# Two places of one recurrent block exchanged: the first norm's statistics go to ScalarE, the bonus goes back to a product of its own

## The chip, the cores and the metric

The program runs on one core of one Trainium2 chip. The metric is device time in microseconds (us) of one execution; times are medians of several runs. The engines are called as the profile calls them: PE (TensorE, with PEld for its weight loads), DVE (VectorE), ACT (ScalarE), POOL (GpSimd) and SP (SyncE, which here issues DMAs only).

## The reference

The kernel computes one RWKV-6 block on 32 sequences of 128 tokens and 512 features, all in float32. Cut to what matters:

```python
xn = layernorm(x)                         # the first norm: mean and variance over 512 features
sx = token_shift(xn)                      # previous token minus this one
xxx = tanh((xn + sx*maa_x) @ maa_w1)      # five small projections
x5 = xn + sx*(maa_stack + xxx @ maa_w2)   # five mixed inputs
w = exp(-exp(time_decay + tanh(x5[1] @ decay_w1) @ decay_w2))
r, k, v, g = x5[3] @ Wr.T, x5[0] @ Wk.T, x5[2] @ Wv.T, silu(x5[4] @ Wg.T)
for t in tokens:                          # 32 heads of 16 x 16 state
    a = k_t[:, None] * v_t[None, :]
    out_t = r_t @ (u * a + s)             # u*a is the "bonus" of the present token
    s = a + w_t[:, None] * s
x = x + (head_norm(out) * g) @ Wo.T
# then a second layernorm, token shift and a squared-ReLU feed-forward with a sigmoid gate
```

## The kernel before, in words

The 32 sequences are worked in eight groups of four (NG = 8, GB = 4), so a group has 512 token columns (N). Each group passes through these streams, which are Python generators:

- front_mix: loads x, runs the first norm (layernorm_T, called with sums None), transposes it on PE, and makes the five mixed inputs x5. The weight products of the mixing are L427, and their evictions are L486 with L488 on POOL, or L491 with L493 on DVE alone.
- front_proj and front_gate: the decay, then k, r, v (matmuls of L408, evictions of L562 on ACT, each with DMAs that put one head's channel on each partition) and the gate (L583 on ACT, L585 on DVE).
- prep: prepares the recurrence on DVE: the rows rk and a10 of the bonus (L660 to L680), the states, and the decays over pairs of tokens. The recurrence steps over pairs of tokens, 64 steps instead of 128.
- The recurrence streams. For each half of the value channels (dh, two of them) and each of the 16 key channels q there is one unit, so 32 units a group: ACT copies the decays into sc (L705) and the start state into a (L716); POOL makes the products am of k and v (L730) and adds them by pairs (L734); DVE runs the scan over time (L768) and multiplies by r into rm (L770); PE adds rm into acc by eight transposing matmuls (L797), a "set". When a half is done, ACT copies acc to y (L811).
- back: head norm, gate and output projection (L885), the sum with x (L894, which also sums rows for the second norm's mean), the second norm (layernorm_T called with sums: a Square pass with an accumulator on ACT, L354, and the normalising pass L368), its transposes and evictions (L394, L384, L905, L908), and the feed-forward (L408 again for its first product, L959, L975).

The statistics of the first norm, for every group, are made on DVE: BN_STATS (L339) and BN_AGGREGATE (L340) for each of the four sequences. After them, for both norms, DVE makes variance plus epsilon (L357, rstd), POOL raises it to the power -0.5 (L359), DVE makes the offset nb (L361), and ACT applies both (L368).

The bonus is made on DVE by bonus_rows: v times rk (L750), v times a10 (L753), and their sum on every second token (L757). In the first and last group the result is a 17th product rm that PE adds as one more set. In groups 1 to 6 ("within") DVE adds it to the rm of the last key channel (L775), so PE has 16 sets for each half.

The order of instructions on each engine is decided when the program is built, by class Plan. It runs all streams together: at each step it takes, among the next operations of all streams that could start earliest by its own estimates (within the tolerance EPSILON), the one with the earliest due time. A stream's due times run in a line from g + v0 to g + v1, and the pairs (v0, v1) stand in DUE. Each operation gives the planner its engine, an estimated duration, and what it reads, writes and allocates; buffers are rings with a few slots (two of rm, two of sc, two of a, one of am, four of blk, four of ps in PSUM). On the chip each engine executes its queue in order, and semaphores make it wait for the others. DMAs are issued on SP's and ACT's queues, so an ACT instruction can stand behind a DMA issue.

Of the kernel before, what the change touches and what calls it, by code (L numbers as in the profile page):

```python
# [10 lines left out]
AF = mybir.ActivationFunctionType  # L11
ALU = mybir.AluOpType
AX = mybir.AxisListType

P = 128
B, L, E = 32, 128, 512
# [4 lines left out]
NG = B // GB  # L21
# [21 lines left out]
LANDING = 2.0  # L43
HOP = (0.2, 0.05, 0.05, 0.04, 0.08)
ON_POOL = (2, 3, 4)
EPSILON = 0.022


DUE = {"rec": (-0.102, 1.125), "mix": (-6.405, -3.209), "proj": (-7.732, 7.646), "gate": (-1.235, 1.547), "prep": (-2.764, -0.303), "back": (-0.938, 3.79), "last1": (-28.476, 2.758), "last2": (7.398, 21.019)}


class Buf:
# [130 lines left out]
def rwkv6_block(ctx: ExitStack, tc: tile.TileContext, x, prev, s0, vecs, u, maa_w1, maa_w2,  # L183
# [94 lines left out]
    def pair(ap):  # L278
        return ap.rearrange("p c (n j) -> p c n j", j=2)
# [46 lines left out]
    def layernorm_T(g, src, sums, vw, vb, which, use, take, need=None, bs=range(GB)):  # L326
# [3 lines left out]

        b0, nb_ = bs[0], len(bs)
        bsl, cols = slice(b0, b0 + nb_), slice(b0 * L, (b0 + nb_) * L)
        if sums is None:
            xh = src
            stats, mv = yield Op(DVE, 0.88, r=[(src, b0)], w=[(0, b0), (1, b0)], alloc=["stats", "mv"])
            for b in bs:
                if b != b0:
                    yield Op(DVE, 0.88, r=[(src, b)], w=[(stats, b), (mv, b)])
                nc.vector.bn_stats(stats[:, b, :], src[:, b, :])  # L339
                nc.vector.bn_aggr(mv[:, b, :], stats[:, b, :])  # L340
            stats.open = False
            mean, var, scale = mv[:, bsl, 0], mv[:, bsl, 1], 1.0
        else:
            mv = sums
            yield Op(DVE, 0.16, r=[(mv, b) for b in bs], w=[(mv, "m")])
            mean, var, scale = mv[:, bsl, 0], mv[:, bsl, 1], 1.0 / E
            nc.vector.tensor_scalar(mean, mean, -1.0 / E, None, ALU.mult)
            xh = None
            for b in bs:
                if xh is None:  # L350
                    (xh,) = yield Op(ACT, 0.83, r=[(src, b), (mv, "m")], w=[(0, b), (mv, ("v", b))], alloc=["ev"])
                else:
                    yield Op(ACT, 0.83, r=[(src, b), (mv, "m")], w=[(xh, b), (mv, ("v", b))])
                nc.scalar.activation(xh[:, b, :], src[:, b, :], AF.Square, bias=mv[:, b, 0:1],  # L354
                                     accum_out=mv[:, b, 1:2])
# [2 lines left out]
        yield Op(POOL, 1.1, r=[(rstd, None)], w=[(rstd, None)], port=True)  # L358
        nc.gpsimd.tensor_tensor(rstd[:, bsl], rstd[:, bsl], mhalf[:, bsl], ALU.pow)  # L359
        (nb,) = yield Op(DVE, 0.16, r=[(mv, None), (rstd, None)], w=[(0, None)], alloc=["nb"], port=True, end=[mv])  # L360
        nc.vector.scalar_tensor_tensor(nb[:, bsl], mean, -1.0 if sums is None else 1.0, rstd[:, bsl], ALU.mult, ALU.mult)  # L361
        for b in bs:
            if g == 0 and sums is None and b % 2:
                yield Op(DVE, 0.5, r=[(src, b), (nb, None), (rstd, None)], w=[(xh, b)], port=True)
# [373 lines left out]
    def rec_dve(gs):  # L738

        for g in gs:  # L740
            d = data[g]
            yield Op(DVE, 0.0, need=lambda: "w01" in d and ("v", "all") in d)
            r, v = d["r"], d["v"]
            r2, v2 = pair(r.t), pair(v.t)
            for dh in range(NDH):
                ds = slice(dh * DH, (dh + 1) * DH)
                def bonus_rows():
                    yield Op(DVE, 0.0, need=lambda: "a10" in d)
                    (rm,) = yield Op(DVE, 1.2, r=[(v, None), (d["rk"], None)], w=[(0, None)], alloc=["rm"], port=True)
                    nc.vector.tensor_tensor(rm.t, v[:, ds, :], d["rk"].t.unsqueeze(1).to_broadcast([P, DH, L]), ALU.mult)  # L750
                    (am,) = yield Op(DVE, 0.67, r=[(v, None), (d["a10"], None)], w=[(0, None)], alloc=["ps"], port=True)
                    bo = am.t.rearrange("p (d n) -> p d n", n=T2)
                    nc.vector.tensor_tensor(bo, v2[:, ds, :, 0], d["a10"].t.unsqueeze(1).to_broadcast([P, DH, T2]),  # L753
                                            ALU.mult)
                    yield Op(DVE, 0.67, r=[(am, None)], w=[(rm, None)], end=[am])
                    rm2 = pair(rm.t)
                    nc.vector.tensor_tensor(rm2[:, :, :, 1], rm2[:, :, :, 1], bo, ALU.add)  # L757
                    return rm

                within = 0 < g < NG - 1  # L760
                for q in range(S):
                    if within and q == S - 1:
                        rows = yield from bonus_rows()
                    yield Op(DVE, 0.0, need=lambda: (g, dh, q, "sum") in unit and (g, dh, q, "sc") in unit)
                    a, sc = unit[g, dh, q, "a"], unit[g, dh, q, "sc"]
                    yield Op(DVE, 1.22, r=[(a, None)], w=[(sc, None)], end=[a])
                    scf = sc.t.rearrange("p d n -> p (d n)")
                    nc.vector.tensor_tensor_scan(scf, scf, a.t.rearrange("p d n -> p (d n)"), 0.0, ALU.mult, ALU.add)  # L768
                    (rm,) = yield Op(DVE, 1.21, r=[(sc, None), (r, None)], w=[(0, None)], alloc=["rm"], end=[sc])
                    nc.vector.tensor_tensor(  # L770
                        pair(rm.t), sc.t.unsqueeze(3).to_broadcast([P, DH, T2, 2]),
                        r2[:, q : q + 1, :, :].to_broadcast([P, DH, T2, 2]), ALU.mult)
                    if within and q == S - 1:
                        yield Op(DVE, 1.2, r=[(rows, None)], w=[(rm, None)], port=True, end=[rows])
                        nc.vector.tensor_tensor(rm.t, rm.t, rows.t, ALU.add)  # L775
                    unit[g, dh, q, "rm"] = rm
                if not within:
                    unit[g, dh, S, "rm"] = yield from bonus_rows()
            r.open = v.open = d["rk"].open = d["a10"].open = False

    def rec_pe(gs):

        for g in gs:
            d = data[g]
            for dh in range(NDH):
                acc = None
                last = S - 1 if 0 < g < NG - 1 else S
                for q in range(last + 1):
                    yield Op(PE, 0.0, need=lambda: (g, dh, q, "rm") in unit)
                    rm = unit[g, dh, q, "rm"]  # L790
                    if acc is None:
                        (acc,) = yield Op(PE, 0.875, r=[(rm, None)], w=[(0, None)], alloc=["acc"], end=[rm])
                    else:
                        yield Op(PE, 0.875, r=[(rm, None)], w=[(acc, None)], end=[rm])
                    for i in range(DH):

                        nc.tensor.matmul(acc[:, i, :], lhsT=rm[:, i, :], rhs=by_head, is_transpose=True,  # L797
                                         start=(q == 0 and i % 4 == 0), stop=(q == last), skip_group_check=True)
                unit[g, dh, "acc"] = acc

    def rec_out(gs):
# [234 lines left out]
```

## Time and profile before

| | us |
|---|---|
| median of three runs | 1539.01 |
| lowest and highest run | 1536.59, 1539.5 |
| profiled execution, own time | 1536.59 |
| its span, first to last instruction | 1534.8 |
| PE busy in the span | 1401.9 (91%) |
| DVE busy | 1276.1 (83%) |
| POOL busy | 1033.6 (67%) |
| ACT busy | 650.9 (42%) |

The profile is one execution, and its times are from the span's start. The mean granted clock of PE was 0.96. "Busy" of PE includes matmuls that overlap in its pipeline, so means of one matmul are longer than the distance between two of them. Register, semaphore and DMA-issuing instructions are not counted as busy.

### The profile page before, as it was taken

The page shows a single profiled execution, that of the slowest core. Times are in us where ns is not written, and L with a number is a line of the kernel's source. Part 1 is how long each engine was busy: PE and PEld are TensorE (multiplying, and loading weights), DVE is VectorE, ACT ScalarE, POOL GpSimd, SP SyncE. Part 2 cuts the span into 40 slices and gives each one's busy share as a digit, 9 for nine tenths or more (in the row PEclk, how much of TensorE's full clock was granted, in tenths as well). Part 3 has the DMA queues.
Part 4 walks back from the last instruction along what each step waited for, and adds up shares of the span by engine and source line. Part 5 has one row for each costly group of instructions (what it writes and reads, how often), then busy time and mean ns, then how long its engine had stood idle before and what let it go on. Part 6 is the DMA issues. An engine that isn't in the chain of part 4 may idle for free.

```text
span 1534.8 us, 16413 instructions
## 1 busy us (share of the span) xinstructions
PE 1401.9 (91%) x5248; PEld 736.2 (48%) x5248; DVE 1276.1 (83%) x1626; ACT 650.9 (42%) x1271; POOL 1033.6 (67%) x642
## 2 busy tenths in 40 slices
PE   5897898889999999999999989999899989779778
PEld 2344454454544555454544545455544555355444
DVE  6529899889989899989989888989989898978742
ACT  3243252324733265434633265424743354245252
POOL 4227895784868958685868949586876959579600
PEclk9998998799999999999999999999999999889889
DMA  6121421343315421442205430243314420410220
GB/s 223 55 86 36 130 69 32 129 128 99 103 32 171 145 89 42 134 137 89 103 31 169 147 123 1 89 149 122 110 32 136 152 87 37 153 40 28 100 65 28
DMA packets 127878, 147.02 MB, mean 96 GB/s; under 512 B 8368, under 2 KB 77616, under 8 KB 126768
## 3 DMA queue, kind: packets, MB, share of 16 engines
q1 hardware_dynamic: 91312, 127.59, 25.2%
q10 hardware_dynamic: 36480, 18.39, 4.2%
q8 instruction: 41, 0.67, 0.2%
q14 instruction: 45, 0.37, 0.1%
HBM read 94.57 MB, written 17.83 MB: 73 GB/s over the span
## 4 chain that ended last, share of the span: by engine, by line
PE 65%; DVE 14%; POOL 4%; ACT 2%; issue 2%; DVEq 0%; ACTq 0%; POOLq 0%
PE ps L408 25%; PE acc L797 11%; PE ps L885 7%; PE ps L975 6%; PE ps L959 6%; PE ps L427 5%; DVE sc L768 3%; POOL am L730 2%; DVE rm L770 2%; PE ps L465 1%; PE ps L414 1%; POOL a L734 1%; PE ps L394 1%; PE ps L865 1%; DVE ps L753 1%
## 5 line engine op out<-in xcount | busy, mean ns | idle before, releaser
L730 POOL TENSOR_TENSOR am<-v,k 128x1024 f32<-128x1024 f32 x256 | 623.2, 2434 | 33.5 <-DMA r<-blk 15.5
L408 PE MATMUL ps<-mx,wt 128*128 128x512 f32 (+1 forms) x1312 | 587.7, 596 | 12.1 <-DVE mx L493 3.7
L734 POOL TENSOR_TENSOR a<-am 128x504 f32<-128x504 f32 x256 | 271.7, 1061 | 220.6 <-DVE sc L768 196.1
L408 PEld LDWEIGHTS ps<-mx,wt 128*128 128x128 f32 x1312 | 245.5, 195 | 281.4 <-issue 252.0
L768 DVE TENSOR_TENSOR_SCAN sc<-sc,a 128x512 f32<-128x512 f32 x256 | 313.1, 1223 | 33.0 <-POOL a L734 28.2
L770 DVE TENSOR_TENSOR rm<-sc,r 128x1024 f32<-128x1024 f32 x256 | 312.4, 1220 | 33.7 <-PE acc L797 22.4
L797 PE MATMUL acc<-by_head,rm 128*128 128x128 f32 x2080 | 278.0, 284 | 44.2 <-DVE rm L770 34.9
L797 PEld LDWEIGHTS acc<-by_head,rm 128*128 128x128 f32 x2080 | 241.6, 146 | 139.4 <-issue 48.2
L705 ACT COPY sc<-w 128x512 f32<-128x512 f32 x256 | 151.5, 592 | 276.8 <-DVE rm L770 226.1
L488 POOL TENSOR_TENSOR mx<-mx,xnT 128x512 f32<-128x512 f32 x94 | 112.2, 1199 | 76.1 <-DVE mx L486 76.1
L716 ACT COPY a<-st 128x8 f32<-128x8 f32 x256 | 52.0, 203 | 164.9 <-DVE sc L768 155.0
L959 PE MATMUL ps<-wt,mx 128*128 128x512 f32 x256 | 116.2, 596 | 3.9 <-ACT blk L535 3.9
L885 PE MATMUL ps<-wt,mx 128*128 128x512 f32 x256 | 113.3, 599 | 0.5 <-DVE mx L876 0.3
L975 PE MATMUL ps<-wt,ev 128*128 128x512 f32 x224 | 101.8, 597 | 5.4 <-DVE mx L493 2.7
L359 POOL TENSOR_TENSOR rstd<-rstd,mhalf 128x4 f32<-128x4 f32 (+1 forms) x17 | 19.4, 1141 | 118.2 <-DVE rstd L357 117.8
L427 PE MATMUL ps<-tha,w2p 64*128 64x512 f32 x256 | 86.0, 678 | 12.2 <-DVE mx L493 5.2
L562 ACT COPY blk<-ps 128x512 f32<-128x512 f32 x96 | 56.1, 584 | 93.2 <-PE ps L408 85.6
L486 DVE SCALAR_TENSOR_TENSOR mx<-ps,vec,sx 128x512 f32<-128x512 f32 x94 | 69.0, 740 | 24.1 <-PE ps L427 24.0
L491 DVE SCALAR_TENSOR_TENSOR ps<-ps,vec,sx 128x512 f32<-128x512 f32 x66 | 49.7, 754 | 38.8 <-PE ps L427 38.1
L885 PEld LDWEIGHTS ps<-wt,mx 128*128 128x128 f32 x256 | 48.8, 192 | 61.7 <-issue 54.8
L959 PEld LDWEIGHTS ps<-wt,mx 128*128 128x128 f32 x256 | 46.5, 190 | 60.1 <-issue 47.8
L975 PEld LDWEIGHTS ps<-wt,ev 128*128 128x128 f32 x224 | 40.4, 190 | 51.4 <-issue 38.7
(111 smaller groups left out, 1348.3 us busy)
## 6 DMA issues: line engine op xcount, KB each, us to landing
x<-in_x SPq DMA_DIRECT2D x13, 1024.0 KB
wt<-in_wk SPq DMA_DIRECT2D x8, 1024.0 KB
wt<-in_wr SPq DMA_DIRECT2D x8, 1024.0 KB
wt<-in_wg SPq DMA_DIRECT2D x8, 1024.0 KB
dgate<-blk SPq DMA_DIRECT2D x32, 256.0 KB
wt<-in_wo SPq DMA_DIRECT2D x8, 1024.0 KB
wt<-in_fk SPq DMA_DIRECT2D x8, 1024.0 KB
wt<-in_fr SPq DMA_DIRECT2D x8, 1024.0 KB
```

What stands on the lines that cost most here:

```text
L408: nc.tensor.matmul(p, lhsT=w[:, c, e * P : (e + 1) * P], rhs=xin[:, c, cols], start=(c == 0), stop=(c == NE - 1))
L427: nc.tensor.matmul(p.t, lhsT=w[h, :], rhs=t[h, :], start=True, stop=True)
L488: nc.gpsimd.tensor_tensor(bt(x5[:, f, :]), bt(x5[:, f, :]), row(xnT, f, 1), ALU.add)
L705: nc.scalar.copy(sc.t, d["w01"][:, q : q + 1, :].to_broadcast([P, DH, T2]))
L730: nc.gpsimd.tensor_tensor(am.t, v[:, ds, :], k[:, q : q + 1, :].to_broadcast([P, DH, L]), ALU.mult)
L734: nc.gpsimd.tensor_tensor(a[:, :, 1:T2], am2[:, :, 0 : T2 - 1, 0], am2[:, :, 0 : T2 - 1, 1], ALU.add)
L768: nc.vector.tensor_tensor_scan(scf, scf, a.t.rearrange("p d n -> p (d n)"), 0.0, ALU.mult, ALU.add)
L770: nc.vector.tensor_tensor(pair(rm.t), sc.t.unsqueeze(3).to_broadcast([P, DH, T2, 2]), r2[:, q : q + 1, :, :].to_broadcast([P, DH, T2, 2]), ...
L797: nc.tensor.matmul(acc[:, i, :], lhsT=rm[:, i, :], rhs=by_head, is_transpose=True, start=(q == 0 and i % 4 == 0), stop=(q == last), skip_g ...
L885: nc.tensor.matmul(p.t, lhsT=att[:, c, b * L : (b + 1) * L], rhs=wot[:, c, :], start=(c == 0), stop=(c == NE - 1))
L959: nc.tensor.matmul(p.t, lhsT=xr[:, c, b * L : (b + 1) * L], rhs=frt[:, c, :], start=(c == 0), stop=(c == NE - 1))
L975: nc.tensor.matmul(p2.t, lhsT=kv[:, c, b * L : (b + 1) * L], rhs=fvt[:, c, :], start=(c == 0), stop=(c == NE - 1))
```

## The change

Three things change.

1. In groups 1 to 7 the statistics of the first norm are made on ACT: for each sequence one pass with AF.Identity and an accumulator (the sum), then one small DVE product that makes the negative mean of all four, then for each sequence a pass with AF.Square, the negative mean as bias, and an accumulator (the sum of squared differences). The passes write a scratch buffer xh, one of the four blk slots, that is read by nobody. Group 0 keeps BN_STATS on DVE.
2. The bonus is the 17th product, with its own set of eight matmuls on PE, in all groups; the DVE add to the last key channel's product is gone.
3. EPSILON and all pairs in DUE have other values, so the planner puts the instructions of all engines in another order.

The diff, cut to its core:

```diff
-EPSILON = 0.022
+EPSILON = 0.0784
-DUE = {"rec": (-0.102, 1.125), "mix": (-6.405, -3.209), "proj": (-7.732, 7.646), "gate": (-1.235, 1.547), "prep": (-2.764, -0.303), "back": (-0.938, 3.79), "last1": (-28.476, 2.758), "last2": (7.398, 21.019)}
+DUE = {"rec": (0.026, 0.93), "mix": (-3.979, -2.846), "proj": (-9.769, 14.248), "gate": (-1.553, 1.011), "prep": (-5.411, 0.831), "back": (-0.15, 3.099), "last1": (-40.499, -0.352), "last2": (-7.951, 22.323)}
...
-        if sums is None:
+        if sums is None and g > 0:
+            xh = None
+            for b in bs:
+                if xh is None:
+                    xh, mv = yield Op(ACT, 0.9, r=[(src, b)], w=[(0, b), (1, b)], alloc=["blk", "mv"])
+                else:
+                    yield Op(ACT, 0.9, r=[(src, b)], w=[(xh, b), (mv, b)])
+                nc.scalar.activation(xh.t, src[:, b, :], AF.Identity, accum_out=mv[:, b, 0:1])
+            mean, var, scale = mv[:, bsl, 0], mv[:, bsl, 1], 1.0 / E
+            yield Op(DVE, 0.16, r=[(mv, b) for b in bs], w=[(mv, "m")])
+            nc.vector.tensor_scalar(mean, mean, -1.0 / E, None, ALU.mult)
+            for b in bs:
+                yield Op(ACT, 0.9, r=[(src, b), (mv, "m")], w=[(xh, b), (mv, ("v", b))], end=[xh] if b == bs[-1] else [])
+                nc.scalar.activation(xh.t, src[:, b, :], AF.Square, bias=mv[:, b, 0:1], accum_out=mv[:, b, 1:2])
+            xh = src
+        elif sums is None:
...
-                within = 0 < g < NG - 1
                 for q in range(S):
-                    if within and q == S - 1:
-                        rows = yield from bonus_rows()
...
-                    if within and q == S - 1:
-                        yield Op(DVE, 1.2, r=[(rows, None)], w=[(rm, None)], port=True, end=[rows])
-                        nc.vector.tensor_tensor(rm.t, rm.t, rows.t, ALU.add)
                     unit[g, dh, q, "rm"] = rm
-                if not within:
-                    unit[g, dh, S, "rm"] = yield from bonus_rows()
+                q = S
...
+                unit[g, dh, q, "rm"] = rm
...
-                last = S - 1 if 0 < g < NG - 1 else S
-                for q in range(last + 1):
+                for q in range(S + 1):
```

## The prediction

> **What bounds the kernel now.** I read the page first, then busy time in ten stretches, cut where the first scan of each group of four sequences starts (115, 287, 464 us and so on), then groups by line, then PE's waits, then the timeline of the start. Columns of the first: length, then PE, PEld, DVE, ACT and POOL busy, granted clock, DMA share, GB/s.
>
> ```profile
> 115.00:287.00 172.00, 147.02 (x566) 74.80 (x566) 154.05 (x188) 59.95 (x127) 126.27 (x78) 0.90 0.22 68
> ...
> 464.00:637.00 173.00, 167.62 (x646) 87.22 (x645) 156.65 (x200) 80.13 (x156) 128.83 (x78) 0.99 0.32 104
> 637.00:811.00 174.00, 168.52 (x653) 87.84 (x651) 157.58 (x200) 80.39 (x157) 128.83 (x78) 0.99 0.32 104
> ...
> 1161.00:1323.00 162.00, 153.33 (x574) 82.74 (x573) 141.90 (x166) 63.52 (x126) 128.62 (x77) 0.98 0.30 98
> 1323.00:1447.00 124.00, 101.34 (x424) 63.10 (x422) 103.91 (x112) 52.08 (x104) 101.46 (x60) 0.88 0.21 71
> ```
>
> Groups 1 to 5 are a PE stage: PE idles 5.4 us of 173, and DVE stands close behind with 157 busy. Group 0 (first row) leaves PE 25 us idle, with DVE 18. Group 7 (last row) again leaves PE 22. So a PE microsecond costs a microsecond in the middle and little at the ends; ACT is under half busy everywhere.
>
> The prices come from the groups by line (busy us, mean ns of one, then idle before):
>
> ```profile
> L797 PE MATMUL acc<-by_head,rm 128*128 128x128 f32 x2080 | 278.0, 284 | 44.2 <-DVE rm L770 34.9 <-DVE rm L775 4.0 <-ACT a L716 2.0
> L770 DVE TENSOR_TENSOR rm<-sc,r 128x1024 f32<-128x1024 f32 x256 | 312.4, 1220 | 33.7 <-PE acc L797 22.4
> L775 DVE TENSOR_TENSOR rm<-rm,rm 128x1024 f32<-128x1024 f32 x12 | 25.5, 2123 | 0.2
> L339 DVE BATCH_NORM_STATS2 stats<-x 128x6 f32<-128x512 f32 x32 | 21.4, 669 | 5.6 <-DMA x<-in_x 5.6
> L354 ACT ACTIVATE ev<-x,mv 128x512 f32<-128x512 f32 x32 | 22.6, 709 | 20.7 <-DVE mv L347 20.7
> L354 ACT ACTIVATION_READ_ACCUMULATOR ev<-x,mv 128x1 f32 x32 | 6.0, 188 | 0.0
> ```
>
> L775, the add that is taken out, costs 2.12 us, not the 1.22 of L770 on the same shape. Between 458 and 1156 us (four groups) PE waited for:
>
> ```profile
> PE ps L394 <- DVE rm L757: 7.3, 4, 1.8
> PE ps L394 <- DVE mx L908: 4.2, 4, 1.1
> PE acc L797 <- DVE rm L775: 3.5, 3, 2.2
> PE ps L959 <- ACT blk L535: 3.1, 4, 0.8
> ```
>
> The first three are one place in each group, where the bonus is put together beside the second norm; there the eight matmul rows that follow take 5.2 us instead of 3.6 (granted clock down).
>
> **Removed.** Twelve L775 adds (groups 1 to 6, two head halves each): 12 x 2.12 = 25.5 us of DVE. Statistics of 28 blocks: BN_STATS and AGGREGATE start again every 0.80 us, 28 x 0.80 = 22.4 us of DVE. Added back are seven tiny mean products, 7 x 0.17 = 1.2. DVE falls by 47 us, some 7.5 a group.
>
> **Added to PE.** The bonus product becomes its own set of eight transposing matmuls again, 12 more. Two sets took 1.90 us in the middle (604.19 to 606.09), so one is 0.94: 12 x 0.94 = 11.3 us, 1.9 a group, in the very stage where PE has no room.
>
> **Added to ACT.** 56 passes with an accumulator. The L354 row is the same operation with the same read behind it: they start 0.70 apart (538.92 to 539.62), so 5.6 us a group and 39 in all, on an engine busy 80 of 173. An immediate bias in the first pass could only make it cheaper; L705's copy of the same 512 columns, 0.59, is the lower end.
>
> The Trainium skill speaks against this move: "ScalarE: Activation LUTs", Rules for kernel authors, says to keep simple add-and-multiply work on VectorE. Per block the rows agree (1.40 on ACT against 0.80), but ACT's half-idle rows make that harmless here; by the rule alone, 5.6 more and 3.2 less a group, the sum would lose 2.4 a group, about 17.
>
> **The order moves too.** Due times and the planner's tolerance change, so I priced the changed kernel's PE order with before's durations: four 128x512 matmuls 3.43 (24 rows in 10.30), a half-height pair 1.06, a split product 1.9, a transpose 0.118, a set 0.94. PE work, before then after: to the first set of group 1, 204.1 and 215.5; group 1, 164.5 and 163.9; groups 2 to 5, 165.5 and 167.4 each; group 6, 147.9 and 137.4; the rest, 149.4 and 152.8; all, 1328.0 and 1339.2. From group 1's first set on, the work left is the same (1123.9 and 1123.7): the 11.3 us are bought ahead, while PE idles in group 0.
>
> **Step 1, to group 1's first scan (287 us).** At the start DVE stood in the way:
>
> ```profile
> 27.33 0.70 DVE L339 BATCH_NORM_STATS2 stats<-x 128x6 f32<-128x512 f32 x1 [2.30 <-DMA x<-in_x]
> ...
> 34.67 0.76 DVE L491 SCALAR_TENSOR_TENSOR ps<-ps,vec,sx 128x512 f32<-128x512 f32 x1
> ```
>
> Eight statistics of groups 1 and 2 sit in front of group 0's mixing, whose matmuls began at 30.50. After, four first passes stand among the three tanh of group 0 on ACT, and they too wait for x until 27.33: three passes, tanh, pass, two tanh end near 31.9 instead of 29.0, and the mixing starts near 33. Queued behind are the second passes and group 2's eight, to about 42, before the next tanh needed at 44.4. Gain some 1.5. Against that, the first scan goes behind bonus products (3.3), two mixing pairs (2.9) and a gate product (0.7); 3.2 of it fits a gap in which DVE idled. DVE work from 115 us to group 1's first scan is 163.1 against 160.5. Net +1, from -2 (all in idle gaps) to +5 (all late).
>
> **Step 2, group 1.** 176.7 us is 12.2 over PE's work. With DVE work 154.8 instead of 165.1 I take 10 over: 174, -2.7 (from -6 to +2).
>
> **Step 3, groups 2 to 5.** 697.5 us now. PE adds 4 x 1.9 = 7.6. DVE's waits in the list above give back between nothing and all: the four groups' DVE waits and clock dips are some 6.5 a group, 26. I take 1.5 a group, 6, since L775 names 0.9 a group and half a dip follows it, while L757 and L908 stay. Net +1.6, from -19 to +7.6.
>
> **Step 4, group 6.** Its first sixteen units hold PE 90.8 and DVE 90.6 now, 79.3 and 82.2 after: -8. The second half keeps its length, since there POOL sets it (a unit every 3.55 us, 1262.91 to 1266.46) and POOL's work doesn't change. -8, from -11 to -4.
>
> **Step 5, group 7 and the tail.** DVE work 156.9 and 158.3, the last 59.7 of PE work alike; 3.4 more PE work falls where PE idles 22. +1, from -3 to +4.
>
> Sum: 1 - 2.7 + 1.6 - 8 + 1 = -7.1. The profiled execution took 1536.59 (span 1534.8 and 1.8 around it), so it would be 1529.5; it is the quickest of three runs, 2.4 under their median, so on the median's scale 1539.0 - 7.1 = 1532.
>
> The page "Perfetto Trace Analysis", Identifying the Most-Contended Engine, says matmul busy time misleads and LDWEIGHTS busy share is the better measure; here that is 48%, which would leave PE room and make the twelve sets free in the middle, 7.6 less, 1524. The waits decide: matmul rows follow each other 0.43 apart with no gap over whole groups, so I charge them.
>
> **Rivals.** *ACT's queue becomes late (slower).* From the last output-projection matmul of groups 1 to 5, DVE now has the first norm's rstd and nb side by side and waits for POOL's power (1.14, up to 2.43 more behind a product); on ACT the fourth Square of the second norm stands behind the four normalising passes that need that nb (2.9), and sc copies, evictions and their DMA issues (1.43 a pair) behind those. I count 17 to 20 us until the transposes of norm 2 can start. PE's cover is 1.9 + 3.43 + 0.94 + 6.86 + 0.94 + 3.43 = 17.5. Late by 2.4, with the clock dip of 1.6, it costs 4 a group, 20 over five: 1552. It decides from 1.4 a group, where the gain of 7 is gone. For it: in before the same chain already ends a microsecond or two late. Against: ACT has 93 idle us a group. *PE paid in full (slower).* The work bought ahead in group 0 delays its DVE-bound scans and nothing comes back: 1539 + 11.3 = 1550. *DVE's relief is whole (faster).* Step 3 at its low end: 1532 - 20 = 1512. *Nothing to see:* relief, ahead-buying and the twelve sets cancel within 0.2%, 3.1 us, about what a measurement can tell from no change.
>
> **How the numbers follow.** Forecast 0.44 (its own range 1523 to 1536), whole relief 0.08, within 0.2% 0.14, ACT late 0.20, PE paid 0.14. Faster 0.52, same 0.14, slower 0.34. The range from 1516 to 1552 takes in half of the whole relief and the stated price of both slower cases, leaving out the rest of each.
>
> **What would show it.** Right: DVE busy near 1230; the stretch of group 6 near 153; groups 2 to 5 at 173 to 175; no wait for L775's place; PE idle in group 0 under 18. Wrong: groups 2 to 5 over 178 with PE waiting at the transposes of norm 2 for ACT's normalising pass, or group 0 several us longer, or group 6 still at 161.

## The result and the profile after

The changed kernel takes 1591.36 us (median of four runs, 1589.20 to 1595.34) against 1538.05 for the kernel before in the same session: a ratio of 1.035, with a 95% interval of 1.033 to 1.037. It is slower by 53 us, where 7 us faster was forecast, and lies 39 us above the upper end of the range. Its profiled execution took 1589.2, with a span of 1587.4, so it is 52.6 over the profiled execution of before, and the stages below can be set side by side.

Lines of code behind the diff are higher by 16 in the first half of the file: L797 is now L803, L354 is L370, the mixing evictions L486, L488 and L491 are L502, L504 and L507. The scan (L768) and rm (L770) keep their numbers. First the busy time by stage, cut again where the first scan of each group starts (same columns as before: length, PE, PEld, DVE, ACT, POOL, granted clock, DMA share, GB/s):

```profile
0.00:122.00 122.00, 94.68 (x260) 39.56 (x260) 52.98 (x86) 53.96 (x102) 35.51 (x37) 0.90 0.37 115
122.00:306.80 184.80, 158.95 (x573) 82.12 (x573) 161.01 (x186) 59.13 (x124) 134.98 (x84) 0.83 0.24 75
...
479.50:661.70 182.20, 171.85 (x665) 91.34 (x664) 153.88 (x191) 86.56 (x172) 126.22 (x78) 0.98 0.31 101
661.70:845.10 183.40, 173.26 (x665) 91.63 (x664) 153.82 (x191) 86.52 (x172) 126.17 (x78) 0.97 0.30 99
...
1207.90:1366.90 159.00, 149.00 (x564) 82.27 (x563) 133.47 (x158) 61.95 (x123) 120.51 (x73) 0.97 0.29 93
1366.90:1493.70 126.80, 104.55 (x436) 65.22 (x435) 104.71 (x113) 52.71 (x105) 100.23 (x60) 0.89 0.19 66
```

The first scan comes 7 us later, group 0 is 12 us longer, and the steady groups (2 to 5) take 182 instead of 174. In these groups DVE is busy for less time than before (154 against 157) and PE idles 10 to 11 us instead of 5 to 8. PE's busy time is some 4 us longer, of which two more sets account for 1.9. So no engine ran out of time: they wait for each other more.

The groups by line show where PE waits (busy, mean ns, then the idle time before them by releaser):

```profile
L803 PE MATMUL acc<-by_head,rm 128*128 128x128 f32 x2176 | 294.1, 285 | 66.8 <-DVE rm L770 59.2 <-DVE rm L784 3.5 <-ACT a L732 2.1
L777 DVE TENSOR_TENSOR rm<-v,rk 128x1024 f32<-128x1024 f32 x16 | 28.0, 1753 | 0.3 <-PE acc L803 0.3
L347 ACT ACTIVATE blk<-x,mv 128x512 f32<-128x512 f32 x28 | 20.2, 722 | 23.4 <-DVE mv L344 22.7
L341 ACT ACTIVATE blk<-x 128x512 f32<-128x512 f32 x28 | 17.6, 630 | 10.4 <-DMA x<-in_x 9.7
```

The single set kept its price (285 ns a matmul against 284). The passes took a little more than forecast: they start again every 0.75 us (L341) and 0.85 us (L347) instead of 0.70. What grew is the idle time in front of the sets: 66.8 us where before had 44.2. PE's waits in the four steady groups (480 to 1210 us), largest first:

```profile
PE acc L803 <- DVE rm L770: 16.9, 12, 1.7
PE ps L410 <- DVE mx L914: 13.6, 8, 2.0
PE ps L981 <- DVE mx L502: 3.4, 4, 0.8
PE ps L443 <- DVE mx L502: 3.4, 4, 0.8
```

L757 and L775, the bonus beside the second norm, are gone from this list, as the change intended. In their place PE waits for the ordinary rm of the recurrence, and more than before for the evictions of the second norm. At the same time DVE waits for PE in front of the feed-forward's last products (DVE's waits, same window):

```profile
DVE ps L970 <- PE ps L981: 25.2, 12, 4.4
DVE sc L768 <- POOL a L750: 19.0, 20, 2.0
DVE mx L502 <- PE ps L443: 16.6, 16, 2.1
```

In before (464 to 1161 us) the rows for the first of PE's waits and the first of DVE's were almost nothing:

```profile
PE acc L797 <- DVE rm L770: 0.7, 2, 0.5
DVE ps L964 <- ACT a L716: 1.1, 4, 0.3
```

The other two waits of DVE are not new: in before DVE waited 14.5 us for POOL at the scan, and 22.9 us for PE in front of the mixing's evictions (L486 and L491).

And the start, where the passes of ACT stand in the timeline (start, us, engine, line, idle before it):

```profile
27.98 0.63 ACT L341 ACTIVATE blk<-x 128x512 f32<-128x512 f32 x1 [3.93 <-DMA x<-in_x]
...
31.90 0.76 DVE L507 SCALAR_TENSOR_TENSOR ps<-ps,vec,sx 128x512 f32<-128x512 f32 x1 [0.40 <-PE ps L443]
...
40.22 0.17 DVE L344 TENSOR_SCALAR mv<-mv 128x4 f32<-128x4 f32 x1 [3.68 <-ACT blk L341]
...
41.83 0.69 PE L430 MATMUL ps<-mx,dw_sb 128*64 128x256 f32 x2 [4.12 <-DVE mx L509]
```

The mixing starts at 31.90, earlier than the 34.67 of before. But the mean product of group 2 (L344) stands in DVE's queue in the middle of it and waits 3.68 us for ACT's passes, with the rest of the mixing behind it and PE behind that. PE's clock falls to half in its gap of 4.12 us and stays there from 39 to 46 us, so the matmuls behind the gap are slow as well.

### The profile page after: what moved, and what is told of

The parts are those of the page before. It is cut to its first block, busy times and chain, and to the rows that moved or that the text cites. A ratio compares the mean times of both kernels' runs of the same rounds, so it can differ in the third digit from the quotient of the medians.

```text
span 1587.4 us, 16643 instructions
## 1 busy us (share of the span) xinstructions
PE 1430.2 (90%) x5344; PEld 759.5 (48%) x5344; DVE 1253.8 (79%) x1565; ACT 694.3 (44%) x1383; POOL 1022.8 (64%) x642
## 4 chain that ended last, share of the span: by engine, by line
PE 58%; DVE 20%; POOL 10%; issue 5%; ACT 4%; DMA 2%; SPq 0%; ACTq 0%; POOLq 0%; DVEq 0%
PE ps L424 21%; PE acc L803 9%; PE ps L981 6%; POOL am L746 6%; PE ps L891 6%; PE ps L965 6%; PE ps L443 6%; DVE sc L768 4%; DVE rm L770 3%; POOL a L750 3%; DVE mx L502 2%; PE ps L430 2%; PE ps L481 2%; PE ps L410 1%; POOL mx L504 1%
## 5 line engine op out<-in xcount | busy, mean ns | idle before, releaser
L746 POOL TENSOR_TENSOR am<-v,k 128x1024 f32<-128x1024 f32 x256 | 613.4, 2396 | 33.7 <-DMA r<-blk 15.6
L803 PE MATMUL acc<-by_head,rm 128*128 128x128 f32 x2176 | 294.1, 285 | 66.8 <-DVE rm L770 59.2
L768 DVE TENSOR_TENSOR_SCAN sc<-sc,a 128x512 f32<-128x512 f32 x256 | 313.3, 1224 | 39.0 <-POOL a L750 37.8
L803 PEld LDWEIGHTS acc<-by_head,rm 128*128 128x128 f32 x2176 | 254.6, 146 | 173.8 <-DVE rm L770 93.8
L770 DVE TENSOR_TENSOR rm<-sc,r 128x1024 f32<-128x1024 f32 x256 | 312.7, 1221 | 30.5 <-PE acc L803 16.7
L504 POOL TENSOR_TENSOR mx<-mx,xnT 128x512 f32<-128x512 f32 x94 | 115.0, 1235 | 126.8 <-DVE mx L502 122.5
L981 PE MATMUL ps<-wt,ev 128*128 128x512 f32 x224 | 105.1, 614 | 3.4 <-DVE mx L502 3.4
L443 PE MATMUL ps<-tha,w2p 64*128 64x512 f32 x256 | 91.7, 690 | 12.7 <-DVE mx L502 5.9
L502 DVE SCALAR_TENSOR_TENSOR mx<-ps,vec,sx 128x512 f32<-128x512 f32 x94 | 68.1, 742 | 31.9 <-PE ps L443 31.8
L507 DVE SCALAR_TENSOR_TENSOR ps<-ps,vec,sx 128x512 f32<-128x512 f32 x66 | 49.6, 751 | 30.0 <-PE ps L443 29.8
```

The source lines that it names most:

```text
L443: nc.tensor.matmul(p.t, lhsT=w[h, :], rhs=t[h, :], start=True, stop=True)
L504: nc.gpsimd.tensor_tensor(bt(x5[:, f, :]), bt(x5[:, f, :]), row(xnT, f, 1), ALU.add)
L746: nc.gpsimd.tensor_tensor(am.t, v[:, ds, :], k[:, q : q + 1, :].to_broadcast([P, DH, L]), ALU.mult)
L770: nc.vector.tensor_tensor(pair(rm.t), sc.t.unsqueeze(3).to_broadcast([P, DH, T2, 2]), r2[:, q : q + 1, :, :].to_broadcast([P, DH, T2, 2]), ...
L981: nc.tensor.matmul(p2.t, lhsT=kv[:, c, b * L : (b + 1) * L], rhs=fvt[:, c, :], start=(c == 0), stop=(c == NE - 1))
```

## The experiments

Two theories stood against each other. **The operations**: the ACT passes and the twelve sets cost more than they free. **The order**: the planner's new tolerance and due times put the queues in an order in which the engines wait for each other, whatever the operations are. The planner runs when the program is built, so an order can be held fixed: the yielded operations stay as they are, and only the instructions issued at them change. Each run below was timed beside the kernel before (medians of 1537 to 1538.5).

**Due times and operations exchanged freely.** Four kernels with one part of the change undone or done alone, planned anew.

```diff
 # f1: the kernel before with the new EPSILON and DUE
 # f2: the changed kernel with the old EPSILON and DUE
 # f3: the changed kernel with BN_STATS on DVE again (new EPSILON and DUE)
 # f4: the changed kernel with the DVE add of the bonus again (new EPSILON and DUE)
```

> The kernel before with only the new EPSILON and DUE: statistics on DVE, bonus added by DVE. Three theories of the 53 us. Order (the new due times put the engines' queues in a worse order, whatever the operations): 1575 to 1595. Statistics (ACT's in-order queue waits for DVE between the two passes and makes scan, evictions and second norm late): 1530 to 1545, as nothing of it is here. Bonus set (PE is full and pays for twelve more sets and the clock that falls after each stall): 1530 to 1545.

Measured: 1640.48 (ratio 1.067, 1.065 to 1.069).

> The changed kernel with the old EPSILON and DUE: statistics on ACT, bonus as a set on PE. Order: 1530 to 1555, most of the 53 us gone. Statistics: 1580 or more, since all passes are there. Bonus set: 1570 or more.

Measured: 1670.43 (1.087, 1.085 to 1.089).

> The changed kernel with the statistics back on DVE in all groups; bonus set and new due times stay. Order: 1585 to 1605 (as slow, or slower, as DVE has 22 us more). Statistics: 1540 to 1555. Bonus set: 1575 to 1595.

Measured: 1601.44 (1.042, 1.039 to 1.045).

> The changed kernel with the bonus added by DVE in groups 1 to 6 again; statistics on ACT and new due times stay. Order: 1575 to 1595. Statistics: 1575 to 1590. Bonus set: 1540 to 1560, as the twelve sets are gone.

Measured: 1662.19 (1.081, 1.079 to 1.083).

Each of the four is slower than both kernels, by 10 to 133 us. The first and the last lie outside all three ranges, the second fits only the two that were open upwards, and the third fits the order's. They don't price the parts, since each gives the planner another order; what they say is that a new plan can move the time by more than any part was thought to cost. So the order had to be frozen.

**The order of before, frozen.** First all operations of the change in the places of the old ones (the extra set is that of the last channel once more, so the bonus itself is not added):

```diff
-                nc.vector.bn_stats(...); nc.vector.bn_aggr(...)
+                nc.scalar.activation(scratch, src[:, b, :], AF.Identity, accum_out=mv[:, b, 0:1])
...
+            (mean product and four Square passes, ahead of rstd)
...
-                        nc.vector.tensor_tensor(rm.t, rm.t, rows.t, ALU.add)
...
+                    times = 2 if q == S - 1 and last == S - 1 else 1
```

> The order of before, kept as planned for before's operations, but the operations of the changed kernel put into its places: statistics by ACT passes where BN_STATS stood, the twelve DVE adds left out, and the last set of each half in groups 1 to 6 issued twice instead (so the bonus itself is left out there and the last channel counts twice; the work is the changed kernel's). Order theory (the operations are nearly neutral, the queues' order is what costs): 1525 to 1550. Operations theory (ACT passes and sets cost the 53 us wherever they stand): 1575 or more.

Measured: 1550.65 (1.008, 1.006 to 1.010), a little over the order theory's range and far from the other. The same operations cost 40.7 us less than in the changed kernel's order (1591.36). Then the statistics alone, and the bonus alone (the rows are added by a set of their own behind the last channel's):

> The order of the kernel before, the bonus as before, and only the statistics of groups 1 to 7 moved: at the places of BN_STATS and BN_AGGREGATE stand the Identity passes, at the place of rstd the mean product and the Square passes. With both exchanges in that order the time was 1550.7, 13 over before, and 10 of it lay before the first scan. Theory A (the passes at the start are the price, the twelve sets are paid for by the relief of DVE): 1547 to 1551, with the start at 125 us and groups 1 to 6 as in before or 0.5 shorter each. Theory B (the sets cost and the passes are harmless): 1538 to 1541.

Measured: 1552.26 (1.009, 1.007 to 1.012), 1 us over theory A, and with the start at 124.8.

```diff
-                        nc.vector.tensor_tensor(rm.t, rm.t, rows.t, ALU.add)
+                        unit[g, dh, "rows"] = rows
...
+                    parts = [rm, unit[g, dh, "rows"]] if 0 < g < NG - 1 and q == last else [rm]
+                    for n, part_ in enumerate(parts):
```

> The order of the kernel before, BN_STATS on DVE as before, and only the bonus exchanged: in groups 1 to 6 the add of the bonus rows on DVE is not issued, and PE adds the rows as a set of their own right behind the set of the last key channel. Both exchanges in that order took 1550.7, the statistics alone 1552.3. Theory A (the relief of DVE pays for the twelve sets, as the forecast had it): 1535 to 1540, groups 1 to 5 each 0 to 1.5 longer and group 6 3 shorter. Theory B (PE paid in full): 1547 to 1550.

Measured: 1537.76 (ratio 0.9999, 0.9988 to 1.0009). In this order the bonus exchange costs nothing, and the statistics on ACT cost as much alone (13.8 us) as both exchanges together (13.4). These passes stand in places that were planned for BN_STATS, and in the kernel with both exchanges DVE waits 18.7 us for them ahead of the first scan, so this is their price in these places. It falls mostly at the start (first row), while a steady group and group 6 (last two rows) look as the forecast had them; busy time by stage of the kernel with both exchanges in the old order:

```profile
0.00:125.00 125.00, 90.74 (x248) 38.43 (x248) 47.83 (x76) 52.68 (x100) 36.36 (x37) 0.88 0.36 112
...
477.30:652.50 175.20, 170.79 (x666) 90.18 (x665) 150.15 (x192) 86.56 (x173) 128.84 (x78) 0.98 0.32 103
1179.10:1337.20 158.10, 150.29 (x573) 81.91 (x572) 135.95 (x164) 62.41 (x125) 127.44 (x77) 0.99 0.30 100
```

**The order of after, frozen, with work left out.** Once without the twelve sets, once without the 56 passes, once without both:

```diff
+                    last = S - 1 if 0 < g < NG - 1 else S
+                    if q > last:
+                        continue
...
-                nc.scalar.activation(xh.t, src[:, b, :], AF.Identity, accum_out=mv[:, b, 0:1])
...
-                nc.scalar.activation(xh.t, src[:, b, :], AF.Square, bias=mv[:, b, 0:1], accum_out=mv[:, b, 1:2])
```

> The changed kernel in its own order, with the twelve bonus sets of groups 1 to 6 not issued on PE (their bonus is left out of the result). If PE is the bound and the sets are paid in full: 1591 - 11 = 1580. If each also tips the clock: 1565 to 1575. If PE has idle time that hides them: 1588 to 1592.

Measured: 1584.25 (1.030): 7 less, against 11.3 us of PE work taken out, so the sets are neither hidden nor paid in full.

> The changed kernel in its own order, with the 56 passes on ACT not issued and the seven mean products replaced by a memset (the first norm's statistics of groups 1 to 7 are left out). Statistics theory (DVE stands behind the mean product, ACT's queue is late for scan and evictions): 1560 or less, 4 us of it at the start, where DVE waited 3.7 us for the passes. Order theory: 1580 to 1591.

Measured: 1584.72 (1.029), as the order theory had it: 7 less, all of it before the first scan, which comes at 115.1 us instead of 122.1. With both left out:

> The changed kernel's order with both kinds of added work left out: the Identity and Square passes of groups 1 to 7 and the twelve bonus sets of groups 1 to 6 are not issued (the statistics are constants and the bonus is not added), and DVE has neither BN_STATS nor the add of the bonus there either, so that less is done than in either kernel. One of the two left out gave 1584.3 and 1584.7. Theory A (the order alone costs some 40): 1574 to 1580, groups 2 to 5 at 180 to 183. Theory B (the sets and the passes cover for each other, and without both the order is as good as the one of before): under 1560.

Measured: 1575.93 (1.024, 1.022 to 1.026), theory A. This kernel does less than either of the two, and less than the kernel before (which has the statistics and the adds on DVE), and still takes 38 us more than before. Its group 0 and a steady group:

```profile
115.40:299.20 183.80, 155.07 (x573) 78.97 (x573) 157.00 (x186) 59.09 (x124) 135.27 (x84) 0.86 0.24 76
654.30:835.00 180.70, 171.55 (x650) 89.43 (x649) 152.93 (x191) 80.62 (x156) 126.16 (x78) 0.98 0.31 100
```

Side by side: in the old order 1538 with before's operations and 1551 with the changed ones, in the new order 1576 with neither and 1591 with the changed ones. The order costs 38 to 41, the operations 13 to 15. By stage (us, profiled executions, cut at the first scans):

| | before | after | all, old order | statistics, old order | bonus, old order | bare, new order |
|---|---|---|---|---|---|---|
| to the first scan | 114.9 | 122.1 | 125.0 | 124.8 | 115.2 | 115.4 |
| group 0 | 172.4 | 184.8 | 173.7 | 173.7 | 172.0 | 183.8 |
| group 1 | 176.7 | 172.8 | 178.6 | 179.0 | 178.2 | 172.8 |
| groups 2 to 5 | 697.5 | 728.4 | 701.8 | 699.8 | 698.0 | 724.8 |
| group 6 | 161.3 | 158.9 | 158.1 | 161.2 | 158.1 | 158.5 |
| group 7 and tail | 212.0 | 220.4 | 212.1 | 211.6 | 212.1 | 218.3 |

**Which part of the new order?** Four kernels keep the changed kernel's queues, but for one or two. Two take work that stood at the head of a queue, in the recurrence's way, and issue it one step later: POOL's mixing adds, and DVE's last products of the feed-forward; a third does both.

```diff
 # POOL: the add L504 is held, and issued behind the next pairwise add L750
+                    plan.hold([x5, xnT], add)
...
 # DVE: L970 and L972 and the store are held, and issued behind the next scan and rm
+                later(gated)
+                later(summed)
+                later(stored)
```

> All operations and PE's, DVE's and ACT's queues as in the changed kernel. Only on POOL, each mixing add of groups 1 to 7 (mx <- mx, xnT) that stood in front of a pairwise add of the recurrence is issued behind the next one instead (not later than the first matmul that reads it). In the changed kernel POOL waited 60 us over four groups for the DVE half of these adds, 30 in before. Theory A (these waits stop the recurrence and are what makes groups 2 to 5 of the changed kernel 8 us longer): groups 2 to 5 at 174 to 177, the total at 1555 to 1570. Theory B (the loss is spread over the whole order): groups 2 to 5 at 180 to 183, total 1583 to 1592. Theory C (the adds become late for PE's projections): over 1592, with PE waiting for mx.

Measured: 1598.04 (1.037, 1.034 to 1.040), groups 2 to 5 at 182 to 184.

> All operations and PE's, ACT's and POOL's queues as in the changed kernel. Only on DVE, the two last products of a block's feed-forward in groups 1 to 5 (ps <- th, ps and x <- ps, x, with the store of x behind them) are issued behind the next unit of the recurrence (scan and rm) instead of in front of it. In the changed kernel DVE stood 25.2 us over four groups in front of the first of them, waiting for PE, 1.1 in before. Theory A (this wait, in front of the scans, is what makes groups 2 to 5 longer): groups 2 to 5 at 176 to 178, the total at 1565 to 1578. Theory B (spread over the order): within 5 us of 1591. Theory C (the ps slots come free later and PE pays): over 1595.

Measured: 1600.24 (1.041, 1.039 to 1.042), groups 2 to 5 at 180 to 184.

> Both moves together: POOL's mixing adds behind the next pairwise add, and DVE's last products of the feed-forward behind the next unit. Theory A (two knots that add up): 1545 to 1562, groups 2 to 5 near 173. Theory B (spread over the order): 1580 to 1592. Theory D (both release the same group end, and one of them is enough): as the better of the two alone.

Measured: 1602.70 (1.042, 1.040 to 1.043). No theory A in any of the three. The totals are 7 to 11 over the changed kernel (the first one's interval still overlaps the changed kernel's), above what theory B allowed. The first two lie in theory C's ranges, but not by its reason: in the first, PE's list has no wait for POOL's mx, and in the second PE's waits over four groups are as long as before the move (42 us against 41).

The first run decides less than it was meant to, because the move did not take POOL's wait away. It was 60.4 us in the changed kernel, and here, over four groups:

```profile
POOL mx L521 <- DVE mx L519: 57.3, 16, 8.7
```

In the second run the wait did go. DVE's waits over four groups show what became of it:

```profile
DVE mx L519 <- PE ps L460: 41.0, 20, 6.2
```

The 25.2 us at L970 are gone, and the next wait for PE (L502 in the changed kernel, here L519) went from 16.6 to 41.0: 41.8 together in the changed kernel, 41.0 here. DVE was not held up by that instruction; it was ahead of PE, and waits for it at the next place. So I turned to PE's queue. In the changed kernel nine of a steady group's 34 sets start within 1 us of the product they add, and in before three or four of 32 in three of the four groups; the median distance is 1.85 against 2.4 to 3.0 us. The fourth kernel issues each set of groups 1 to 6 one item later:

```diff
+                        plan.flush()
+                        plan.hold([rm, acc], added)      # issued behind the next other item on PE
```

> All operations and DVE's, ACT's and POOL's queues as in the changed kernel. Only on PE, each set of groups 1 to 6 (acc <- by_head, rm) is issued behind the next item of other work instead of in front of it. In the changed kernel nine sets of a group's 34 started within 1 us of the product rm that they add, and the median distance was 1.85 us, against four of 32 and 2.7 us in before; PE waited 16.9 us over four groups for rm, 4.2 in before. Theory A (PE's order, with the sets too close behind their products, is what makes groups 2 to 5 longer): groups 2 to 5 at 174 to 178, total 1560 to 1578. Theory B (the loss is spread over the order): 180 to 183, total 1583 to 1595. Theory C (DVE then waits for the two rm slots): over 1597, with DVE waiting at rm for PE.

Measured: 1630.59 (1.060, 1.058 to 1.062), groups 2 to 5 at 188 to 190. Theory C: PE hardly waits for rm any more (4.7 us over four groups instead of 16.9), but rm has two slots, and now DVE waits for PE to empty them (DVE's waits of this kernel, four groups):

```profile
DVE rm L789 <- PE acc L822: 54.3, 28, 5.2
```

The median distance from product to set is 4.5 us here. A set too early makes PE wait, a set too late makes DVE wait.

**The clock in group 0.** Near the end of group 0 in the changed kernel PE has little but a set every 2.5 to 3.5 us, and its clock falls to half (busy time in steps of 10 us; the clock is the third number from the end):

```profile
260.00:270.00 10.00, 5.94 (x25) 4.74 (x25) 8.49 (x7) 2.51 (x7) 9.53 (x7) 0.54 0.00 1
270.00:280.00 10.00, 6.86 (x25) 4.56 (x26) 8.61 (x9) 2.81 (x7) 9.61 (x6) 0.50 0.16 51
280.00:290.00 10.00, 8.42 (x21) 4.01 (x19) 7.01 (x9) 4.14 (x7) 7.95 (x5) 0.50 0.26 74
290.00:300.00 10.00, 8.32 (x17) 3.50 (x16) 4.32 (x7) 0.43 (x2) 4.56 (x4) 0.50 0.72 256
```

The kernel before has a dip in this place too (half clock from 259 to 269 and from 276 to 293 us, 27 us against 44). The next kernel issues the last sets of group 0 three times, so that PE has something to do (which adds those sets up threefold):

```diff
+                    times = 3 if g == 0 and dh == 1 and q >= 4 else 1
```

> The changed kernel in its own order, with the last sets of group 0's second half (from its fifth channel on) issued three times each, so that PE has more work there (these sums count three times in the result). Clock theory (PE, short of work there, runs 44 us at half clock, and the mixing of the next group behind it runs slowly too): faster by 6 to 12, near 1582, though PE has 25 sets more to do. Without it: 1591 to 1605, the sets' own price.

Measured: 1591.21 (1581.46 to 1592.88; ratio 1.033). In its profiled execution the clock stays at 1.00 to the end of the group, group 0 takes 180.8 instead of 184.8 and the span is 1579.6, 8 less, although PE does 26 sets more (13 sets, two more times each). But that execution is the fastest of the four, 10 us under the other three, and the median is that of the changed kernel, as without the clock theory. Whether the dip costs anything in most executions is left open.

**How rough is it?** Two last kernels change nothing but EPSILON, by a step that is small against the change's own (0.022 to 0.0784).

```diff
-EPSILON = 0.022        # the kernel before
+EPSILON = 0.03
...
-EPSILON = 0.0784       # the changed kernel
+EPSILON = 0.07
```

> All operations and due times of the kernel before; only the planner's tolerance EPSILON is 0.03 instead of 0.022, which moves some instructions in every queue. Theory A (the time hangs on the order in a rough way, so that an order made from other numbers is tens of us worse or better, whatever the operations): over 1550. Theory B (orders near each other cost the same, and what counts is the operations): 1533 to 1545.

Measured: 1631.99 (1.061, 1.059 to 1.063).

> All operations and due times of the changed kernel; only EPSILON is 0.07 instead of 0.0784. The same step on the kernel before (0.03 instead of 0.022) gave 1632.0, 94 over. Theory A (rough on this side too): more than 15 away from 1591, more likely above. Theory B (the changed kernel's order lies on a plateau): 1583 to 1599.

Measured: 1606.28 (1.044, 1.041 to 1.047). The first is 94 us over the kernel before (1538.05) with exactly its operations. The second is 15 over the changed kernel, just between its two theories. Two stages of the first, a group of the old length beside one of 195:

```profile
482.90:657.80 174.90, 167.04 (x641) 89.02 (x641) 151.74 (x195) 80.96 (x157) 120.89 (x71) 0.98 0.29 91
657.80:853.00 195.20, 175.26 (x649) 91.64 (x650) 166.44 (x205) 80.65 (x156) 137.42 (x87) 0.95 0.31 103
```

With nothing added and nothing removed, a step of 0.008 in one number costs 94 us on the one side and 15 on the other. The 40 us of the changed kernel's order are nothing special beside that.

**A version that beats both.** In the old order group 6 gained 3 us by the bonus exchange and no other stage gained. So one more: the kernel before, with the exchange in group 6 alone.

```diff
-                        nc.vector.tensor_tensor(rm.t, rm.t, rows.t, ALU.add)
+                        if g == NG - 2:
+                            unit[g, dh, "rows"] = rows
+                        else:
+                            nc.vector.tensor_tensor(rm.t, rm.t, rows.t, ALU.add)
```

> The order of the kernel before, and the bonus exchanged in group 6 alone, where PE is not the bound: with both exchanges in that order group 6 took 158.0 instead of 161.3. Theory A: 3 less than before, 1534 to 1536, and everything but group 6 as in before. Theory B (the 3 were something else): 1537 to 1539.

Measured: 1534.07 against 1536.96: the medians are 2.9 us apart, and the ratio over all runs is 0.9975 (0.9965 to 0.9984). It is a small gain, but clear of the noise. Group 6 in its profile takes 157.8 instead of 161.3:

```profile
991.10:1164.60 173.50, 166.61 (x650) 87.03 (x649) 157.28 (x201) 79.99 (x157) 128.78 (x78) 1.00 0.32 104
1164.60:1322.40 157.80, 149.30 (x564) 81.51 (x563) 136.12 (x164) 62.36 (x125) 127.49 (x77) 0.99 0.30 100
```

The row above group 6 is group 5, which takes 173.5 as in before. The spans of the two profiled executions are equal (1534.8), because in this one group 1 took 179.9 instead of 176.7; so the gain is read from the medians, of 12 and 23 runs.

## Why the prediction was wrong

**What failed.** The sum took each stage as the work of its busiest engine plus the waits that before had there, and let the new order in only through PE's work. PE's work was counted right. The term that failed is the waits and clock dips of groups 2 to 5: they were forecast 6 us shorter than in before, and they came out some 23 us longer. PE idles 41.9 us in these four groups instead of 25.5, and it runs at half clock for 23.8 us instead of 10.2, which is some 7 us of work lost. The waits belong to the order, and no step priced the new order's waits. Step 3's bounds (-19 to +7.6) only let them shrink or stay.

**Step 1 (+1 forecast, +19.6 measured).** Two errors. The start was forecast to gain 1.5 and lost 7.2, of which 7.0 are the passes' (the kernel without them has its first scan at 115.1). The times were nearly right: the mixing began at 31.90, against "near 33", and group 2's second passes ended near 44, against "about 42". What was missed is that the mean product is an instruction of DVE, in front of group 0's mixing in DVE's queue. I asked who waits for the passes on ACT, and not what stands behind the mean product on DVE. PE's queue is the same in the kernel without passes, so the two can be set side by side: behind this wait PE is 3.8 us late (at 41.83), 5.7 at 46.14, after the stretch at half clock, and 7.0 at 80.15, after a second one. Group 0 lost 12.4, of which 11 remain without sets and passes (183.8): the order. Two parts of it can be seen: DVE's busy time in group 0 rose from 154 to 161, where work of 2.6 more was counted, and PE ran 61 us at half clock there, against 35 in before.

**Work bought ahead.** The claim that 11.4 us of PE's work moves ahead of group 1's first set is right as a count: before that set the trace has 280 matmuls of 128x512 in the projections instead of 256, and 136 instead of 132 of 64x512, which is 11.4 us at the prediction's prices. But the work was not bought with idle time. The set came at 315.0 instead of 293.7, and what followed, the same amount of work by that count, took 31 us more.

**Step 2 (-2.7 forecast, -3.9 measured)** was right in sign and size, but this looks like luck. In the old order group 1 has the relief of DVE too, and takes 178 to 179, longer than before. And the gain hangs on where the stage is cut: from PE's first set of group 1 to that of group 2 it is 179.0 instead of 175.7.

**Step 3 (+1.6 forecast, +30.9 measured)** holds most of the miss. The +7.6 for the sets was sound as work (PE's counted work rises by 1.9 a group), and in the old order the exchange as a whole cost nothing there: groups 2 to 5 changed by +0.5 (697.5 to 698.0). The place of L757 and L775 in PE's waits was the right one, and they went. But the -6 for the waits became +23, as said above. The order's part is 27 (724.8 in the bare kernel).

**Step 4 (-8 forecast, -2.4 measured).** The relief of DVE is shown (in the old order group 6 gains 3 by the exchange alone), the rest of the 8 is not: 10.5 us of PE's work did leave the group (147.9 to 137.4, as counted), but its stretch between scans shrank by only 2.4. **Step 5 (+1 forecast, +8.4 measured)**: 6.3 of it are in the bare kernel too.

**DVE's busy time** was to be 1230 and is 1253.8. In the old order the same operations give 1231 (the sum of the busy times by stage), so the count was right; the new order made the same instructions longer (below).

**The rivals.** ACT's queue was not late: PE's waits at the second norm's transposes are for DVE's evictions (13.6 us over four groups), and no wait of PE for the normalising pass is in the list. PE paid in full named the place (group 0's scans are delayed and nothing comes back), but its price, 11.3, is far from what it took. The case that decided was not among the rivals: an order that is worse by itself. The front of the document held what spoke for it: the planner's tolerance and eight pairs of due times had changed, and every queue with them. The operations alone, 13 us in the old order, would have ended just inside the range's upper end.

**What stays open.** Why this order costs 8 us in each steady group is not settled by naming one queue. By the account of PE's time, the 31 us of groups 2 to 5 are 16 of idle time, 8 of added sets and 7 of half clock; this says where they fall, not what starts them. Moving DVE's products did not help, and the wait that was removed came back elsewhere in full; moving PE's sets made it worse; moving POOL's adds did not remove their wait, so that place stays untested.

## What to carry to other kernels

When a change comes with new numbers for a scheduler, price the order apart from the operations, and give it a range of its own, which can be far wider than anything that the operations can do: freeze the old order and put the new operations in, and freeze the new order and take them out. A wait that stands first in a list is worth its length only if nothing else is late behind it, which is tried by moving that instruction alone and adding up the waits again. For every instruction that is moved between engines, look also at the small one that stays behind as the link: here a product of 0.17 us held DVE's queue for 3.7.

## What the runs showed of the hardware

A DVE product of two SBUF operands can take more than four times its length beside POOL. In group 0 of the changed kernel the bonus product, 1.21 us at its shortest, took 5.51 while POOL ran two adds, a product and half of a pairwise add almost without a break (timeline):

```profile
195.04 2.32 POOL L504 TENSOR_TENSOR mx<-mx,xnT 128x512 f32<-128x512 f32 x2
195.24 5.51 DVE L777 TENSOR_TENSOR rm<-v,rk 128x1024 f32<-128x1024 f32 x1
197.31 2.36 POOL L746 TENSOR_TENSOR am<-v,k 128x1024 f32<-128x1024 f32 x1
...
199.75 1.89 POOL L750 TENSOR_TENSOR a<-am 128x504 f32<-128x504 f32 x1
```

The longest of before was 2.95. Added up, DVE's instructions last 1317.9 us in the changed kernel and 1300.0 for the same operations in the old order. That POOL is the cause is read from these rows and was not tried by itself. The Trainium skill, "SBUF — State Buffer", section "SBUF: two separate sides", says that the two engines hold a shared pair of ports for a whole instruction and the other one is blocked; the rows agree that the DVE product is held up, and add that more than one POOL instruction in a row passed it.

The clock of PE fell to 0.50 at about 261 us and stayed there to 305, though no wait of PE in that stretch, or in the 10 us ahead of it, was longer than 1.6 us; being busy 60 to 85% at half clock did not raise it. More transposing matmuls kept it from falling: with the sets issued three times it stayed at 1.00, through 168 of them in a row (258.17 to 276.73 us). "TensorE: Matmul & The Clock Gate" gives a gap of some 3 us as what brings the clock down (section "Why this matters for your kernels") and says of transposes that they don't count as PE's work in the same way (Part 4); here both measurements differ, and they decide.
